# First layer's loop on Trainium2: K^T V over token tiles, with V taken inside or behind the loop, and gate logits per tile or per four tiles

## The chip, the core and the metric

The kernel runs on one core of one Trainium2 chip. The metric is device time in microseconds (us) of one execution, as the median of several runs. A core has five engines[...]: TensorE (PE in the profile, its weight loads PEld), VectorE (DVE), ScalarE (ACT), GpSimd (POOL) and SyncE (SP). They meet through semaphores. In this kernel SP issues nearly all DMA transfers. SBUF is the on-chip memory with 128 partitions, PSUM the accumulators that TensorE writes[...].

## The reference, cut to what matters

Two transformer layers over 2048 tokens of width 512, all in float32. The change lies in the first layer, in what is summed over all tokens before its main stage can start:

```python
xn = _layernorm(x)
k = heads(xn @ k_w.T + k_b);  v = heads(xn @ v_w.T + v_b)      # 16 heads of 32
kp = elu(k) + 1
kv = einsum('bhsd,bhse->bhde', kp, v)                          # sums over tokens
z  = einsum('bhsd,bhd->bhs', qp, kp.sum(axis=2))
attn = einsum('bhsd,bhde->bhse', qp, kv) / (z + EPS)
probas = sigmoid(x2 @ Wg.T)                                    # 16 experts, x2 = xn
_, idx = top_k(probas + biases, 8)
```

Linear attention needs one 32x32 matrix per head (kv) and the sum of kp. The mixture of experts needs, per token, the 8 highest of 16 gates. Only kv's diagonal blocks (a head with itself) are used, so the kernel computes a 128x128 block for four heads and multiplies it with a block-diagonal mask. Because v is linear in xn, the sum over tokens of kp^T v equals (sum of kp^T xn) V^T plus (sum of kp)^T v_b.

## The kernel before

Tokens are cut into NT = 16 tiles of P = 128; D = 512 is cut into NC = 4 chunks of 128; TB = 512 tokens make one of NTB = 4 blocks. Python code emits the instructions; a scheduler of the framework orders them per engine by its own estimates, and tile pools with a fixed number of buffers add the waits for a buffer's last reader. So the order on an engine is not exactly that of the source.

The first stage is the loop `for t in range(NT)` (L194 to L266). Per tile:

- VectorE takes layernorm statistics for four tiles ahead (`stats`, L72, L73, L76, L77) and writes xn (L224). GpSimd adds the output bias ob to x (L228), and SP stores that to DRAM as the residual.
- TensorE transposes xn in four pieces (tr, L100); ScalarE copies the result to xnT (L107).
- TensorE forms pk = xn K^T (L236): four matmuls of 512 columns. The profile counts eight, since each float32 matmul is issued twice here. VectorE adds the bias (kk, L238), takes min(kk, 0) (ke, L252), ScalarE takes the exponential (L253), VectorE forms elu + 1 (kk again, L254).
- TensorE forms pv in the same way (L241); VectorE adds its bias into vv (L244), which has a column of ones behind each group of 128, set by GpSimd (L243).
- TensorE forms pg (L257), gate logits with 16 columns, and adds kk^T vv to four PSUM accumulators kv of 128x129 (L259); the last column collects the sum of kp.
- `experts_of` turns the logits into a sigmoid and into each expert's rank among the 16: three short operations (L180, L181, L183) and five of 256 elements (L188 to L192) on VectorE.

Behind the loop VectorE masks kv into bd and the sums into bdz (L270 to L273). Then a new stage opens with other PSUM pools: query projections (pq, L305), a latent projection (pl, L329), the expert weights from the ranks (`expert_weights`), transposes of the weights (wp, L376), and `folded`, which multiplies bd with the output weights. A PSUM bank can be taken by the new stage when its old tile has been read.

[...]four banks for kv, two for tag "mm" (pk, pv), two for tag "tr" (tr, pg). Working SBUF tiles (xn, kk, ke and so on) have two buffers each, x has eight. SP's queue takes the loads in the order of the source: x of tile 0, k_wT, x of tile 1, kb, v_wT, vb, x of tile 2, WgT, rb, x of tile 3, ob, then x of tiles 4 to 7 and the weights of the later stages.

Of the kernel before, what the change touches and what calls it, by code (L numbers as in the profile page):

```python
# [19 lines left out]
P = 128  # L20
T = 2048
NT = T // P
# [16 lines left out]
def two_layer_kernel(ctx: ExitStack, tc: tile.TileContext, a: dict, out: bass.AP):  # L39
# [27 lines left out]
    def load(eng, dst, src):  # L67
        eng.dma_start(out=dst, in_=src)
# [34 lines left out]
    def vcopy(o, i):  # L103
        V.tensor_copy(o, i)
# [12 lines left out]
    with ExitStack() as l0:  # L117
# [15 lines left out]
        with ExitStack() as p1:  # L133
            w1 = p1.enter_context(tc.tile_pool(name="w1", bufs=1))
            wk1 = p1.enter_context(tc.tile_pool(name="wk1", bufs=2))
            ps_kv = p1.enter_context(tc.tile_pool(name="ps_kv", bufs=1, space=PSUM))
            ps1 = p1.enter_context(tc.tile_pool(name="ps1", bufs=2, space=PSUM))

            kc = "(c p) o -> p c o"
            x = {}  # L140

            def load_x(t):
                x[t] = wk1.tile([P, D], F32, tag="x", name=f"x_{t}", bufs=8)
                load(nc.sync, x[t], a["x"][t * P : (t + 1) * P, :])


            load_x(0)
            k_wT = weight("k_wT", [P, NC, D], a["k_wT"].rearrange(kc, p=P), w1)
            load_x(1)
            kb = weight("kb", [P, D], a["k_b"].partition_broadcast(P), w1)  # L150
            v_wT = weight("v_wT", [P, NC, D], a["v_wT"].rearrange(kc, p=P), w1)
            vb = weight("vb", [P, D], a["v_b"].partition_broadcast(P), w1)
            load_x(2)
            WgT = weight("WgT", [P, NC, E], a["WgT"].rearrange(kc, p=P))
            rb = weight("rb", [P, E], a["rbias"].partition_broadcast(P), w1)
            load_x(3)
            ob = weight("ob", [P, D], a["o_b"].partition_broadcast(P), w1)
            bmask = const([P, P], "bmask", w1)
            make_block_diagonal(nc, bmask, HD)
            tie = const([P, E, E], "tie", w1)  # L160
            G.memset(tie, 1.0)
            G.affine_select(
                out=tie, in_=tie, pattern=[[1, E], [-1, E]], compare_op=ALU.is_gt, fill=0.0,
                base=0, channel_multiplier=0,
            )
            mv = const([P, NT, 2], "mv", w1)
            rstd = const([P, NT], "rstd", w1)
            def stats(lo, hi):
                for t in range(lo, hi):
                    layernorm_stats(wk1, mv[:, t, :], x[t], f"st_{t}")  # L170
                rsqrt_into(rstd[:, lo:hi], mv[:, lo:hi, 1], eps5)

            stats(0, 1)
            stats(1, 4)

            def experts_of(t, pg):

                V.tensor_scalar_add(prob[:, t, :], pg, 1.0)  # L180
                V.reciprocal(prob[:, t, :], prob[:, t, :])  # L181
                sc = wk1.tile([P, E], F32, tag="sc", name=f"sc_{t}")
                V.tensor_tensor(sc, prob[:, t, :], rb, ALU.add)  # L183
                other = sc.unsqueeze(1).to_broadcast([P, E, E])
                own = sc.unsqueeze(2).to_broadcast([P, E, E])
                gt = wk1.tile([P, E, E], F32, tag="gt", name=f"gt_{t}")
                eq = wk1.tile([P, E, E], F32, tag="eq", name=f"eq_{t}")
                V.tensor_tensor(gt, other, own, ALU.is_gt)  # L188
                V.tensor_tensor(eq, other, own, ALU.is_equal)
                V.tensor_tensor(eq, eq, tie, ALU.mult)  # L190
                V.tensor_tensor(gt, gt, eq, ALU.add)
                V.tensor_reduce(rank[:, t, :], gt, AX.X, ALU.add)  # L192

            kv = [ps_kv.tile([P, P + 1], F32, tag=f"kv{g}", name=f"kv{g}") for g in range(NC)]  # L194
            for t in range(NT):
                tok = slice(t * P, (t + 1) * P)
                xt = xnT[t // 4][:, :, t % 4 * P : (t % 4 + 1) * P]
                if t % 4 == 0 and t + 4 < NT:
                    for u in range(t + 4, t + 8):
                        load_x(u)  # L200
                    stats(t + 4, t + 8)
                if t == 0:
                    q_b = weight("q_b", [P, NC], a["q_b"])

                    q_wT = weight("q_wT", [P, NC, D], a["q_wT"].rearrange(kc, p=P))
                    WdT = weight("WdT", [P, NC, LAT], a["WdT"].rearrange(kc, p=P))
                    sw1T = weight("sw1T", [P, NC, HID], a["sw1T"].rearrange(kc, p=P))
                    swgT = weight("swgT", [P, NC, HID], a["swgT"].rearrange(kc, p=P))
                    rw1T = weight("rw1T", [P, E, HID], a["rw1T"])
                    rwgT = weight("rwgT", [P, E, HID], a["rwgT"])  # L210
                    rw2T = weight(
                        "rw2T", [P, 2, E, LAT], a["rw2T"].rearrange("(b p) e l -> p b e l", p=P)
                    )
                    o_wT = weight("o_wT", [P, NC, D], a["o_wT"].rearrange(kc, p=P))
                    sw2T = weight("sw2T", [P, 2, D], a["sw2T"].rearrange(kc, p=P))
                    WuT = weight("WuT", [P, D], a["WuT"])
                    wr = weight("wr", [P, D], a["w_router"].partition_broadcast(P))
                    for j in range(2):
                        load(
                            nc.sync, w_qk[:, :, j * D : (j + 1) * D],  # L220
                            a["w_qkv"][:, j * D : (j + 1) * D].rearrange(kc, p=P),
                        )
                xn = wk1.tile([P, D], F32, tag="xn", name=f"xn_{t}")
                V.tensor_scalar(  # L224
                    xn, x[t], mv[:, t, 0:1], rstd[:, t : t + 1], ALU.subtract, ALU.mult
                )

                G.tensor_tensor(x[t], x[t], ob, ALU.add)  # L228
                load(nc.sync, res_d[tok, :], x[t])
                transpose4(  # L230
                    ps1, lambda c: xn[:, c * P : (c + 1) * P], xt, f"tr_{t}", scopy
                )

                pk = ps1.tile([P, D], F32, tag="mm", name=f"pk_{t}")
                for c in range(NC):
                    PE.matmul(pk, xt[:, c, :], k_wT[:, c, :], start=c == 0, stop=c == NC - 1)  # L236
                kk = wk1.tile([P, D], F32, tag="kk", name=f"kk_{t}")
                V.tensor_tensor(kk, pk, kb, ALU.add)  # L238
                pv = ps1.tile([P, D], F32, tag="mm", name=f"pv_{t}")
                for c in range(NC):  # L240
                    PE.matmul(pv, xt[:, c, :], v_wT[:, c, :], start=c == 0, stop=c == NC - 1)  # L241
                vv = wk1.tile([P, NC, P + 1], F32, tag="vv", name=f"vv_{t}")
                G.memset(vv[:, :, P : P + 1], 1.0)  # L243
                V.tensor_tensor(  # L244
                    vv[:, :, 0:P],
                    pv.rearrange("p (g e) -> p g e", g=NC),
                    vb.rearrange("p (g e) -> p g e", g=NC),
                    ALU.add,
                )

                ke = wk1.tile([P, D], F32, tag="ke", name=f"ke_{t}")
                V.tensor_scalar_min(ke, kk, 0.0)  # L252
                S.activation(ke, ke, AF.Exp)  # L253
                V.scalar_tensor_tensor(kk, kk, 0.0, ke, ALU.max, ALU.add)  # L254
                pg = ps1.tile([P, E], F32, tag="tr", name=f"pg_{t}")
                for c in range(NC):
                    PE.matmul(pg, xt[:, c, :], WgT[:, c, :], start=c == 0, stop=c == NC - 1)  # L257
                for g in range(NC):
                    PE.matmul(  # L259
                        kv[g], kk[:, g * P : (g + 1) * P], vv[:, g, :],  # L260
                        start=t == 0, stop=t == NT - 1,
                    )

                eg = wk1.tile([P, E], F32, tag="eg", name=f"eg_{t}")
                S.activation(eg, pg, AF.Exp, scale=-1.0)
                experts_of(t, eg)  # L266


            for g in range(NC):
                V.tensor_tensor(bd[:, g, :], kv[g][:, 0:P], bmask, ALU.mult)  # L270
                ks = wk1.tile([P, 1], F32, tag="ks", name=f"ks_{g}")
                vcopy(ks, kv[g][:, P : P + 1])
                V.tensor_scalar_mul(bdz[:, g, :], bmask, ks)  # L273

        with ExitStack() as p3:
# [1030 lines left out]
```

## Time and profile before

| what | value |
|---|---|
| median of 3 runs | 1873.57 us (1873.55 to 1880.08) |
| profiled execution, its own time | 1869.43 us |
| span in the profile | 1867.7 us |
| mean granted clock of TensorE | 0.97 |
| first loop, first transpose to last kv | 7.1 to 161.5 us |
| VectorE busy from 100 to 155 us | 37.7 of 55 us |
| ScalarE busy from 100 to 155 us | 8.3 of 55 us |
| GpSimd busy from 100 to 155 us | 5.3 of 55 us |
| first query projection of the next stage starts | 162.89 us |

The profile shows one execution. A timeline row gives start, length, engine, line of the kernel, operation, output and inputs, shapes and a count; in brackets stands how long the engine was idle before it and which engine's instruction released it. [...]start to start is what a group costs. The span begins with the first instruction and is somewhat shorter than the execution's time.

### The profile page before, as it was taken

The numbers are of one execution on the slowest core, as the hardware profiler recorded it, in microseconds if no ns is written. First come the engines' busy times: TensorE is split into PE (matmuls) and PEld (weight loads), VectorE is DVE, ScalarE is ACT, GpSimd is POOL, SyncE is SP. The second block draws the span as 40 slices with busy tenths as digits, with TensorE's granted clock in tenths as the row PEclk, the third lists the DMA queues.
The fourth block names the chain that finished last, engine by engine and source line by source line (L and its number), as shares of the span: only waits on it lengthen the run. The fifth ranks groups of instructions, "written<-read, shape, count | busy, mean of one in ns | idle before, by whom it ended". The sixth has DMA issues, their size and how long they took to land. (4 is left out here: it accounts for less than half of the span.)

```text
span 1867.7 us, 20604 instructions
## 1 busy us (share of the span) xinstructions
PE 1740.5 (93%) x8120; PEld 767.4 (41%) x8120; DVE 1008.1 (54%) x1445; ACT 573.7 (31%) x923; POOL 497.2 (27%) x372
## 2 busy tenths in 40 slices
PE   7999999999999999868988887999999999999999
PEld 4555444344444333323433333454565333333333
DVE  6775645436445343696666564575555455444344
ACT  3212334233233243111111111142100366446463
POOL 2110000100100110333344431331000467458583
PEclk9999999999999999989999897999999899999999
DMA  9301001210213130100001004311132300110100
GB/s 362 128 29 43 23 28 39 85 34 29 72 53 74 33 109 23 62 23 23 23 23 29 26 12 149 122 51 68 46 111 92 91 1 1 35 57 1 46 1 35
DMA packets 61810, 107.12 MB, mean 57 GB/s; under 512 B 12209, under 2 KB 13745, under 8 KB 61201
## 3 DMA queue, kind: packets, MB, share of 16 engines
q1 hardware_dynamic: 55280, 104.01, 16.7%
q0 software_dynamic: 1152, 1.21, 0.4%
q8 instruction: 63, 1.03, 0.2%
q10 hardware_dynamic: 5280, 0.59, 0.2%
q14 instruction: 35, 0.28, 0.0%
HBM read 84.14 MB, written 21.65 MB: 57 GB/s over the span
## 5 line engine op out<-in xcount | busy, mean ns | idle before, releaser
L527 DVE TENSOR_REDUCE mx<-pa 128x4 f32<-128x1536 f32 (+3 forms) x144 | 252.9, 1756 | 178.2 <-PE pa L523 83.8
L1210 POOL TENSOR_TENSOR acc<-acc,pt 128x1024 f32<-128x1024 f32 (+3 forms) x126 | 253.8, 2047 | 122.1 <-ACT pt L1137 75.8
L1137 ACT ACTIVATE pt<-ps 128x1024 f32<-128x1024 f32 (+3 forms) x208 | 182.2, 923 | 138.1 <-DVE ps L1128 86.4
L515 PE MATMUL pa<-kT,qT 32*128 32x384 f32 (+3 forms) x1152 | 158.0, 562 | 47.5 <-DVE mx L527 39.3
L1104 PE MATMUL ps<-qT,kT 32*128 32x512 f32 (+3 forms) x1152 | 162.0, 535 | 8.6 <-ACT pt L1137 8.1
L93 POOL TENSOR_TENSOR xr<-xr,xn 128x512 f32<-128x512 f32 x16 | 27.0, 1697 | 493.6 <-DVE xn L87 493.6
L424 PE MATMUL acc<-h,rw2T 128*128 128x512 f32 x256 | 135.3, 616 | 14.9 <-DVE h L290 14.3
L288 ACT ACTIVATE r_e<-eg 128x512 f32<-128x512 f32 x128 | 75.8, 594 | 222.4 <-PE eg L419 202.4
L782 PE MATMUL p<-w_qk,xnt 128*128 128x512 f32 x256 | 129.7, 631 | 8.3 <-ACT xnt L107 8.3
L290 DVE TENSOR_TENSOR h<-ea,r_e 128x512 f32<-128x512 f32 x128 | 87.0, 686 | 87.2 <-ACT r_e L289 59.9
L421 PE MATMUL ea<-xw,rw1T 128*128 128x512 f32 x256 | 130.7, 592 | 0.0
L419 PE MATMUL eg<-xl,rwgT 128*128 128x512 f32 x256 | 130.7, 592 | 0.0
L1128 DVE TENSOR_TENSOR ps<-ps,maskT 128x256 f32<-128x256 f32 (+1 forms) x144 | 68.3, 514 | 100.3 <-PE ps L1111 97.2
L1104 PEld LDWEIGHTS ps<-qT,kT 32*128 32x128 f32 x1152 | 62.2, 186 | 116.5 <-issue 55.4
L515 PEld LDWEIGHTS pa<-kT,qT 32*128 32x128 f32 x1152 | 52.0, 191 | 138.3 <-DVE mx L527 88.0
L1177 PE MATMUL av<-pt,v 128*32 128x512 f32 (+3 forms) x1024 | 102.3, 485 | 0.2
L415 DVE TENSOR_TENSOR xw<-xw,xl 128x512 f32<-128x512 f32 x64 | 43.9, 685 | 94.9 <-DMA xw<-w_d 94.9
L1219 DVE RECIPROCAL sm<-sm 128x128 f32<-128x128 f32 x64 | 61.8, 965 | 57.4 <-PE sm L1191 56.0
L424 PEld LDWEIGHTS acc<-h,rw2T 128*128 128x128 f32 x256 | 43.4, 188 | 95.5 <-DVE h L290 79.4
L289 ACT ACTIVATE r_e<-r_e 128x512 f32<-128x512 f32 x128 | 80.2, 629 | 6.4 <-issue 1.9
L650 POOL TENSOR_TENSOR t<-qk,cosg 128x1024 f32<-128x1024 f32 x15 | 35.3, 2354 | 161.7 <-DVE qk L645 145.5
L421 PEld LDWEIGHTS ea<-xw,rw1T 128*128 128x128 f32 x256 | 48.6, 190 | 61.2 <-issue 60.8
(278 smaller groups left out, 2542.2 us busy)
## 6 DMA issues: line engine op xcount, KB each, us to landing
xw<-w_d SPq DMA_DIRECT2D x64, 256.0 KB, 3.2
x<-in_x SPq DMA_DIRECT2D x16, 256.0 KB, 4.3
res_d<-x SPq DMA_DIRECT2D x16, 256.0 KB, 2.3
xr<-res_d SPq DMA_DIRECT2D x16, 256.0 KB, 4.8
xn_d<-xn SPq DMA_DIRECT2D x16, 256.0 KB, 2.4
res_d<-xr SPq DMA_DIRECT2D x16, 256.0 KB, 2.0
xnq<-xn_d SPq DMA_DIRECT2D x16, 256.0 KB, 2.9
v_d<-vt SPq DMA_DIRECT2D x16, 256.0 KB, 2.9
```

Source lines behind the costliest of these rows:

```text
L289: S.activation(r, r, AF.Square)
L290: V.tensor_tensor(dst, pa, r, ALU.mult)
L419: PE.matmul(pg, rwgT[:, e, hb], xl, start=True, stop=True)
L421: PE.matmul(pa, rw1T[:, e, hb], xw, start=True, stop=True)
L424: PE.matmul(acc, rw2T[:, j, e, :], h, start=e == 0 and j == 0, stop=e == E - 1 and j == 1,)
L515: PE.matmul(pS[:, h, : w * P], qT[r, g, i * P : (i + 1) * P], kT[r, g, ks], start=True, stop=not (edge or last),)
L527: V.tensor_reduce(mx[:, g, :, c], pS[:, :, : w * P], AX.X, ALU.max)
L782: PE.matmul(pj, xnt[:, c, :], w, start=c == 0, stop=c == NC - 1)
L1104: PE.matmul(pS[h // 2][:, h % 2, t0 * P - q0 : (t1 + 1) * P - q0], kT[r, g, kb * P : (kb + 1) * P], qT[r, g, t0 * P : (t1 + 1) * P], start ...
L1137: S.activation(pT[:, :, :n], pS[hp][:, :, :n], AF.Exp)
L1177: PE.matmul(self.av[h * HD : (h + 1) * HD, t0 * P - o : (t1 + 1) * P - o], vs[kb // 4][:, kb % 4, hs], got[h // 2][:, h % 2, t0 * P - q0 : ...
L1210: eng.tensor_tensor(part, part, got[hp][:, :, : q1 - q0], ALU.add)
```

## The change

Four things change.

1. The loop no longer forms v. It accumulates gx = kk^T xn, four PSUM tiles of 128x512, over all tiles (`gathered`). A tile's gx is emitted one tile later, behind the next tile's pk. The sum of kp is kept by GpSimd (ksum, one add per tile). xn gets three buffers instead of two.
2. Behind the loop, gx is copied out (gs), transposed (trg, gT) and multiplied with the V weights, only in the 128 columns that a group of four heads needs. ksum's column sum comes from a matmul with a column of ones. The V bias enters as vb times that sum, then the mask.
3. Gate logits come per block of four tiles (`gates`): each of the four chunks of xnT goes through its own group of 32 columns of the array with weights padded from 16 to 32 columns, the four partial sums land on four groups of partitions of one PSUM tile, ScalarE copies them out, and matmuls with a 0/1 matrix `fold` add them up and turn them to tokens on partitions. Sigmoid and bias are then done for four tiles at once, the ranking per tile as before. The gates of the last block are emitted behind the loop.
4. The loads of v_wT and vb move behind x of tile 3; WgT is zeroed by GpSimd first.

```diff
@@ -148,12 +148,15 @@
             k_wT = weight("k_wT", [P, NC, D], a["k_wT"].rearrange(kc, p=P), w1)
             load_x(1)
             kb = weight("kb", [P, D], a["k_b"].partition_broadcast(P), w1)
+            load_x(2)
+
+            WgT = const([P, NC, HD], "WgT", w1)
+            G.memset(WgT, 0.0)
+            load(nc.sync, WgT[:, :, 0:E], a["WgT"].rearrange(kc, p=P))
+            rb = weight("rb", [P, E], a["rbias"].partition_broadcast(P), w1)
+            load_x(3)
             v_wT = weight("v_wT", [P, NC, D], a["v_wT"].rearrange(kc, p=P), w1)
             vb = weight("vb", [P, D], a["v_b"].partition_broadcast(P), w1)
-            load_x(2)
-            WgT = weight("WgT", [P, NC, E], a["WgT"].rearrange(kc, p=P))
-            rb = weight("rb", [P, E], a["rbias"].partition_broadcast(P), w1)
-            load_x(3)
             ob = weight("ob", [P, D], a["o_b"].partition_broadcast(P), w1)
             bmask = const([P, P], "bmask", w1)
             make_block_diagonal(nc, bmask, HD)
@@ -163,6 +166,15 @@
                 out=tie, in_=tie, pattern=[[1, E], [-1, E]], compare_op=ALU.is_gt, fill=0.0,
                 base=0, channel_multiplier=0,
             )
+            ones = const([P, 1], "ones", w1)
+            G.memset(ones, 1.0)
+            ksum = const([P, D], "ksum", w1)
+            G.memset(ksum, 0.0)
+
+            fold = const([P, E], "fold", w1)
+            V.tensor_reduce(
+                fold, ident.rearrange("p (c e) -> p e c", c=4)[:, 0:E, :], AX.X, ALU.add
+            )
             mv = const([P, NT, 2], "mv", w1)
             rstd = const([P, NT], "rstd", w1)
             def stats(lo, hi):
@@ -173,25 +185,53 @@
             stats(0, 1)
             stats(1, 4)
 
-            def experts_of(t, pg):
-
-
-
-                V.tensor_scalar_add(prob[:, t, :], pg, 1.0)
-                V.reciprocal(prob[:, t, :], prob[:, t, :])
-                sc = wk1.tile([P, E], F32, tag="sc", name=f"sc_{t}")
-                V.tensor_tensor(sc, prob[:, t, :], rb, ALU.add)
-                other = sc.unsqueeze(1).to_broadcast([P, E, E])
-                own = sc.unsqueeze(2).to_broadcast([P, E, E])
-                gt = wk1.tile([P, E, E], F32, tag="gt", name=f"gt_{t}")
-                eq = wk1.tile([P, E, E], F32, tag="eq", name=f"eq_{t}")
-                V.tensor_tensor(gt, other, own, ALU.is_gt)
-                V.tensor_tensor(eq, other, own, ALU.is_equal)
-                V.tensor_tensor(eq, eq, tie, ALU.mult)
-                V.tensor_tensor(gt, gt, eq, ALU.add)
-                V.tensor_reduce(rank[:, t, :], gt, AX.X, ALU.add)
-
-            kv = [ps_kv.tile([P, P + 1], F32, tag=f"kv{g}", name=f"kv{g}") for g in range(NC)]
+            def gates(b):
+
+
+
+
+                parts = ps1.tile([P, TB], F32, tag="mm", name=f"pgp_{b}")
+                for c in range(NC):
+                    PE.matmul(
+                        parts[c * HD : (c + 1) * HD, :], WgT[:, c, :], xnT[b][:, c, :],
+                        start=True, stop=True, skip_group_check=True,
+                    )
+                gp = wk1.tile([P, TB], F32, tag="gp", name=f"gp_{b}", bufs=1)
+                scopy(gp, parts)
+                pg = ps1.tile([P, 4, E], F32, tag="tr", name=f"pg_{b}")
+                for i in range(4):
+                    PE.matmul(
+                        pg[:, i, :], gp[:, i * P : (i + 1) * P], fold, start=True, stop=True
+                    )
+
+                four = slice(4 * b, 4 * b + 4)
+                pr = prob[:, four, :]
+                S.activation(pr, pg, AF.Exp, scale=-1.0)
+                V.tensor_scalar_add(pr, pr, 1.0)
+                V.reciprocal(pr, pr)
+                sc = wk1.tile([P, 4, E], F32, tag="sc", name=f"sc_{b}", bufs=1)
+                V.tensor_tensor(sc, pr, rb.unsqueeze(1).to_broadcast([P, 4, E]), ALU.add)
+                for i in range(4):
+                    other = sc[:, i, :].unsqueeze(1).to_broadcast([P, E, E])
+                    own = sc[:, i, :].unsqueeze(2).to_broadcast([P, E, E])
+                    gt = wk1.tile([P, E, E], F32, tag="gt", name=f"gt_{b}_{i}")
+                    eq = wk1.tile([P, E, E], F32, tag="eq", name=f"eq_{b}_{i}")
+                    V.tensor_tensor(gt, other, own, ALU.is_gt)
+                    V.tensor_tensor(eq, other, own, ALU.is_equal)
+                    V.tensor_tensor(eq, eq, tie, ALU.mult)
+                    V.tensor_tensor(gt, gt, eq, ALU.add)
+                    V.tensor_reduce(rank[:, 4 * b + i, :], gt, AX.X, ALU.add)
+
+
+            gx = [ps_kv.tile([P, D], F32, tag=f"gx{g}", name=f"gx{g}") for g in range(NC)]
+
+            def gathered(t, kk, xn):
+                for g in range(NC):
+                    PE.matmul(
+                        gx[g], kk[:, g * P : (g + 1) * P], xn, start=t == 0, stop=t == NT - 1
+                    )
+
+            before = None
             for t in range(NT):
                 tok = slice(t * P, (t + 1) * P)
                 xt = xnT[t // 4][:, :, t % 4 * P : (t % 4 + 1) * P]
@@ -220,7 +260,7 @@
                             nc.sync, w_qk[:, :, j * D : (j + 1) * D],
                             a["w_qkv"][:, j * D : (j + 1) * D].rearrange(kc, p=P),
                         )
-                xn = wk1.tile([P, D], F32, tag="xn", name=f"xn_{t}")
+                xn = wk1.tile([P, D], F32, tag="xn", name=f"xn_{t}", bufs=3)
                 V.tensor_scalar(
                     xn, x[t], mv[:, t, 0:1], rstd[:, t : t + 1], ALU.subtract, ALU.mult
                 )
@@ -236,40 +276,48 @@
                     PE.matmul(pk, xt[:, c, :], k_wT[:, c, :], start=c == 0, stop=c == NC - 1)
                 kk = wk1.tile([P, D], F32, tag="kk", name=f"kk_{t}")
                 V.tensor_tensor(kk, pk, kb, ALU.add)
-                pv = ps1.tile([P, D], F32, tag="mm", name=f"pv_{t}")
-                for c in range(NC):
-                    PE.matmul(pv, xt[:, c, :], v_wT[:, c, :], start=c == 0, stop=c == NC - 1)
-                vv = wk1.tile([P, NC, P + 1], F32, tag="vv", name=f"vv_{t}")
-                G.memset(vv[:, :, P : P + 1], 1.0)
-                V.tensor_tensor(
-                    vv[:, :, 0:P],
-                    pv.rearrange("p (g e) -> p g e", g=NC),
-                    vb.rearrange("p (g e) -> p g e", g=NC),
-                    ALU.add,
-                )
 
                 ke = wk1.tile([P, D], F32, tag="ke", name=f"ke_{t}")
                 V.tensor_scalar_min(ke, kk, 0.0)
                 S.activation(ke, ke, AF.Exp)
                 V.scalar_tensor_tensor(kk, kk, 0.0, ke, ALU.max, ALU.add)
-                pg = ps1.tile([P, E], F32, tag="tr", name=f"pg_{t}")
+                G.tensor_tensor(ksum, ksum, kk, ALU.add)
+                if before is not None:
+                    gathered(*before)
+                before = t, kk, xn
+                if t % 4 == 3 and t < NT - 1:
+                    gates(t // 4)
+            gathered(*before)
+            gs = []
+            for g in range(NC):
+                gs.append(wk1.tile([P, D], F32, tag="gs", name=f"gs_{g}", bufs=4))
+                (vcopy if g % 2 else scopy)(gs[g], gx[g])
+            gates(NTB - 1)
+
+
+
+            def turned_g(g):
+                gT = wk1.tile([P, NC, P], F32, tag="ke", name=f"gT_{g}")
+                transpose4(
+                    ps1, lambda c: gs[g][:, c * P : (c + 1) * P], gT, f"trg_{g}",
+                    scopy if g % 2 else vcopy,
+                )
+                return gT
+
+            gT = turned_g(0)
+            for g in range(NC):
+                cols = slice(g * P, (g + 1) * P)
+                this, gT = gT, turned_g(g + 1) if g < NC - 1 else None
+                kv = ps1.tile([P, P + 1], F32, tag="mm", name=f"kv_{g}")
                 for c in range(NC):
-                    PE.matmul(pg, xt[:, c, :], WgT[:, c, :], start=c == 0, stop=c == NC - 1)
-                for g in range(NC):
                     PE.matmul(
-                        kv[g], kk[:, g * P : (g + 1) * P], vv[:, g, :],
-                        start=t == 0, stop=t == NT - 1,
-                    )
-
-                eg = wk1.tile([P, E], F32, tag="eg", name=f"eg_{t}")
-                S.activation(eg, pg, AF.Exp, scale=-1.0)
-                experts_of(t, eg)
-
-
-            for g in range(NC):
-                V.tensor_tensor(bd[:, g, :], kv[g][:, 0:P], bmask, ALU.mult)
+                        kv[:, 0:P], this[:, c, :], v_wT[:, c, cols], start=c == 0, stop=c == NC - 1
+                    )
+                PE.matmul(kv[:, P : P + 1], ksum[:, cols], ones, start=True, stop=True)
                 ks = wk1.tile([P, 1], F32, tag="ks", name=f"ks_{g}")
-                vcopy(ks, kv[g][:, P : P + 1])
+                vcopy(ks, kv[:, P : P + 1])
+                V.scalar_tensor_tensor(bd[:, g, :], vb[:, cols], ks, kv[:, 0:P], ALU.mult, ALU.add)
+                V.tensor_tensor(bd[:, g, :], bd[:, g, :], bmask, ALU.mult)
                 V.tensor_scalar_mul(bdz[:, g, :], bmask, ks)
 
         with ExitStack() as p3:
```

Around the transposes, the copies and pk nothing changes, nor in any later stage.

## The prediction

> **What bounds the kernel now.** I read the page's busy table first, then TensorE's timeline over the first layer's loop, then VectorE's and GpSimd's, then the hand-over to the next stage.
>
> ```profile
> PE 1740.5 (93%) x8120; PEld 767.4 (41%) x8120; DVE 1008.1 (54%) x1445; ACT 573.7 (31%) x923; POOL 497.2 (27%) x372
> ```
>
> TensorE is busy 93% of the span. One loop tile in its timeline (start, length, engine, line, operation):
>
> ```profile
> 115.10 1.06 PE L259 MATMUL kv<-vv,kk 128*128 128x129 f32 x8
> 116.00 3.64 PE L236 MATMUL pk<-k_wT,xnT 128*128 128x512 f32 x8
> 119.48 3.60 PE L241 MATMUL pv<-v_wT,xnT 128*128 128x512 f32 x8
> 122.91 0.96 PE L257 MATMUL pg<-WgT,xnT 128*128 128x16 f32 x8
> 123.72 0.64 PE L100 MATMUL tr<-ident,xn 128*128 128x128 f32 x4
> 124.19 1.06 PE L259 MATMUL kv<-vv,kk 128*128 128x129 f32 x8
> ```
>
> No row has an idle time in brackets: this loop is bound by TensorE. From start to start: kv 0.90, pk 3.48, pv 3.43, pg 0.81, tr 0.47, together 9.09 us a tile. The loop ends here:
>
> ```profile
> 160.38 1.13 PE L259 MATMUL kv<-vv,kk 128*128 128x129 f32 x8
> 162.89 5.37 PE L305 MATMUL pq<-xnT,q_wT 128*128 128x512 f32 x8 [1.38 <-issue]
> 168.09 3.60 PE L329 MATMUL pl<-xnT,WdT 128*128 128x512 f32 x8
> ```
>
> The next stage starts at 162.89, 1.4 us behind the last kv. Its first group takes 5.2 us instead of 3.43, at a granted clock of 0.68. In a row by windows (busy time of TensorE, its weight loads, VectorE, ScalarE and GpSimd, then clock, DMA share and GB/s):
>
> ```profile
> 163.00:168.30 5.30, 5.30 (x9) 2.27 (x10) 2.90 (x12) 0.00 (x0) 0.00 (x0) 0.68 0.44 134
> ```
>
> On VectorE and GpSimd I read the chain from pk to a finished kk, the gates, and what a GpSimd operation does to them:
>
> ```profile
> 97.87 1.18 DVE L183 TENSOR_TENSOR sc<-prob,rb 128x16 f32<-128x16 f32 x1
> ...
> 137.86 0.69 DVE L238 TENSOR_TENSOR kk<-pk,kb 128x512 f32<-128x512 f32 x1 [0.28 <-PE pk L236]
> 138.59 0.43 DVE L252 TENSOR_SCALAR ke<-kk 128x512 f32<-128x512 f32 x1
> 139.77 0.69 DVE L254 SCALAR_TENSOR_TENSOR kk<-kk,ke 128x512 f32<-128x512 f32 x1 [0.76 <-ACT ke L253]
> ...
> 161.44 0.41 DVE L188 TENSOR_TENSOR gt<-sc 128x256 f32<-128x256 f32 x1
> 161.77 0.42 DVE L189 TENSOR_TENSOR eq<-sc 128x256 f32<-128x256 f32 x1
> ```
>
> ```profile
> 97.75 1.27 POOL L228 TENSOR_TENSOR x<-x,ob 128x512 f32<-128x512 f32 x1 [7.78 <-DVE xn L224]
> ```
>
> From pk's end (137.66) to kk's second write (140.46) is 2.8 us, 2.87 with the signal to TensorE. Independent gate operations follow every 0.33 to 0.34 us, dependent ones every 0.46. The tiny sc took 1.18 us because GpSimd was adding ob; elsewhere (142.87) it takes 0.17.
>
> [...]eight 128x512 instructions of 32 columns, in four groups, follow the eight before them after 0.88 us, where eight full-width ones take 3.43.
>
> ```profile
> 1507.79 1.07 PE L1177 MATMUL av<-acc,v 128*32 128x512 f32 x8
> 1508.67 1.04 PE L1191 MATMUL sm<-acc,ones_f 128*32 128x512 f32 x8
> ```
>
> [...]Here 1.4 us of idle between short matmuls already led to 0.68.
>
> **The loop.** Per tile pv (3.43), kv (0.90) and pg (0.81) go. gx comes: four matmuls kk x xn of 512 columns, priced as pv, 3.43. Per four tiles come four column-group matmuls (0.88, from av) and four fold matmuls (0.81, as pg). So four tiles cost 4 x (0.47 + 3.48 + 3.43) + 0.88 + 0.81 = 31.2 us instead of 36.4: 5.2 a block, 20.6 in four blocks, if TensorE never waits.
>
> Waits, from the built order of instructions, walked with the durations above:
> - The copy of xnT takes 0.7 us from tr's end. Before, kv stood between; now gx's first matmul (0.86) usually does. It doesn't before tiles 5, 9 and 13 (behind a gates block) nor 10: 4 x about 0.8 lost; and pk of tile 1 waits 0.3.
> - The first gx of a tile stands behind three gx and a tr of the next round: 2.57 + 0.47 = 3.04 us, against 2.87 for kk. It just fits; behind it queue pk and everything later.
> - The fold waits for a ScalarE copy (0.7). After blocks 0 and 2 a gx covers it, after block 1 nothing: 0.8.
> - VectorE now gets the gates of four tiles in one piece: add, reciprocal and sc 0.6, then 20 interleaved operations x 0.34 = 6.8. The next tile's kk, ke and the xn two tiles on queue behind. In block 0 gates start near 40.1 and kk of tile 4 near 47.2, while TensorE has gx, tr and pk until 50.5. Then the add of ob (1.27) locks out kk's last operation: ready about 51.1, 0.7 late. The same in block 2. In block 1 four layernorm statistics join, yet xn of tile 10 (about 83.2) still meets its tr (83.9).
> - ksum, 16 new GpSimd adds of 1.27, lies beside other work[...].
>
> New waits sum to 3.2 + 0.3 + 0.8 + 1.4 = 5.7. Old ones were alike: from the end of the first pk (14.47) to the last kv (161.4) are 146.9 us, of which 15 x 9.09 + 5.1 = 141.5 are work, so 5.4 idle, 2.1 of it for the statistics of tiles 1 to 3. Those come earlier now: v_wT and vb (1.25 MB) move behind x of tiles 2 and 3 in SP's queue, so xn of tile 1 is ready near 13, before the first pk ends. x of tiles 4 to 7 has the same transfers ahead as before. The 64 KB of WgT's wider tile is only memory.
>
> After: 15 x (0.47 + 3.48) + 16 x 3.43 + 4 x 0.88 + 0.9 (the last group-matmuls are split around gx) + 3 x 0.81 = 121.0, plus 5.7 = 126.7: the loop ends near 141.2 by this sum, 140.6 in the walk, which charges pk 3.43 to 3.48. I take 140.6: 20.8 us earlier than 161.4.
>
> **The tail takes most of it back.** At 140.6: ScalarE copy and fold to 142.3, Exp to 142.6, add and reciprocal to 143.1, VectorE's copy of the first transposed gx to 143.7. TensorE transposes and does the first two kv by about 146.5. The third kv needs the third transposed copy, and its PSUM buffer back from the first bd. Both stand on VectorE behind 19 gate operations of tiles 12 to 15: 143.9 + 6.5 = 150.4, ks and copy to 151.1, last reduction and bd to 151.7. TensorE is idle about 5 us there, so I charge half clock: kv 3 and 4 take 1.9 us each instead of 1.1 (eight of 0.11 and two for ks), to 155.7. pq starts at once: its bank was a gx bank, long read. I give pq 4.4, between 3.43 (warm by then) and 5.2 (still cold): end 160.1, before 168.1. The expert weights' order behind pq is unchanged, and rank is ready by 154, ahead of its transposes.
>
> Sum: 20.8 - (15.1 - 1.5) + 0.8 = 8.0 us gained (the tail is 15.1 now, 1.5 before; pq is 0.8 shorter). From pq on the order of every engine is the same: the rest only moves. Profiled execution: 1869.43 -> 1861.4, span 1867.7 -> 1859.7. The median of the runs, 1873.57, stands 4.1 higher; I take the same 8.0 off: **1865.6**. A comparison of this kernel can't tell less than about 0.5% (9.4 us) from no change; the forecast lies just inside that.
>
> **Unknown costs.** gx: kk as stationary operand, between pv's 3.43 and 3.48 as pk (0 to 0.8 in sum). Group matmuls: 0.88 to 3.43 if they don't overlap. Tail: half clock costs 0 to 3.4 in all (kv and pq), and the gate step may be 0.46 (+2.3). Lock: [...]some 4 us more if it catches an operation of each block's chain twice.
>
> **Rivals.**
> - Faster: waits behind gates hide, the lock costs nothing, the clock stays up: 8.0 + 1.4 + 1.6 + 1.0 = 12, time 1861.6. For it: the old tail shows only 1.4 us from kv to pq. Against: the order puts the gates ahead of the copy. 0.36 for anything beyond 9.4.
> - Column groups run one after another: 4 x 2.55 = 10.2 lost, time 1875.8. Against it: the av rows, same type and shape. 0.05.
> - Small gain: gates step 0.46 and locks add up: 8.0 - 2.3 - 4 = 1.7, time 1872. 0.12.
> - Slower, one mechanism: kk is late in each tile. Its cover is 0.17 us (3.04 against 2.87). If ksum's and ob's adds, both on GpSimd behind kk and xn, hold ke and kk's last operation in every tile, each lateness counts about 12 times: at 0.84 us the gain is gone, at 1.6 it is slower by 0.5%; both adds in the chain (2.5) give 1893.6. Against: by the walk these adds end before the next pk does. 0.07.
> - The forecast, a gain of 5 to 9.4: 0.40.
>
> Faster 0.36, same 0.57 (forecast, small gain, serial groups), slower 0.07. The range from 1859.5 to 1874 leaves out slower, serial groups and the end of faster. The forecast's own range is 1864 to 1869.
>
> **What would show it.** A tile period near 7.4 between gates, no idle before gx above 0.2 us outside them; the four group matmuls within 1 us; TensorE idle some 5 us before the third kv, released by VectorE's copy of gT; pq starting near 155. Wrong if gx waits for kk in most tiles, or if the next stage starts before 151 or after 160.

## The result

| | before | after |
|---|---|---|
| median of the runs made together | 1873.55 us (1868.85 to 1880.08) | 1863.01 us (1855.82 to 1869.61) |
| profiled execution, its own time | 1869.43 us | 1855.82 us |
| span in the profile | 1867.7 us | 1854.1 us |
| first query projection starts | 162.89 us | 158.56 us |
| latent projection starts | 168.09 us | 162.72 us |
| fold of the output weights (pw) starts | 177.3 us | 172.0 us |

The ratio after to before is 0.994, with a 95% interval from 0.9925 to 0.9955: a gain of 10.5 us, between 8.4 and 14. The forecast was 1865.6 us, a gain of 8.0.

Below, "the fold" as a place in time is the start of pw, the fold of the output weights; the fold inside the loop's gates is the multiplication with the 0/1 matrix. "Half clock" is a stretch in which the profile's record of the granted TensorE clock shows 0.5.

The busy table of the page, after:

```profile
PE 1728.6 (93%) x7984; PEld 749.5 (40%) x7984; DVE 984.0 (53%) x1402; ACT 576.1 (31%) x919; POOL 519.1 (28%) x375
```

TensorE has 136 instructions and 11.9 us of busy time less, VectorE 24.1 us less, GpSimd 21.9 us more (ksum). TensorE's timeline of the changed first stage (start, length, engine, line, operation, and in brackets the idle time before it with its releaser):

```profile
20.65 3.70 PE L230 MATMUL gx<-xn,kk 128*128 128x512 f32 x8 [0.34 <-DVE kk L283]
...
37.68 1.06 PE L195 MATMUL pgp<-xnT,WgT 128*32 128x512 f32 x8
38.68 1.12 PE L230 MATMUL gx<-xn,kk 128*128 128x512 f32 x2
...
56.90 3.68 PE L276 MATMUL pk<-k_wT,xnT 128*128 128x512 f32 x8
60.41 2.74 PE L230 MATMUL gx<-xn,kk 128*128 128x512 f32 x6
62.99 0.60 PE L100 MATMUL tr<-ident,xn 128*128 128x128 f32 x4
63.43 1.04 PE L230 MATMUL gx<-xn,kk 128*128 128x512 f32 x2
64.30 3.66 PE L276 MATMUL pk<-k_wT,xnT 128*128 128x512 f32 x8
...
138.31 3.70 PE L230 MATMUL gx<-xn,kk 128*128 128x512 f32 x8
141.94 1.06 PE L195 MATMUL pgp<-xnT,WgT 128*32 128x512 f32 x6
143.69 1.07 PE L203 MATMUL pg<-fold,gp 128*128 128x16 f32 x8 [0.69 <-ACT gp L107]
...
154.27 2.07 PE L313 MATMUL kv<-v_wT,gT 128*128 128x128 f32 x8 [3.12 <-DVE bd L319]
...
158.56 4.33 PE L353 MATMUL pq<-xnT,q_wT 128*128 128x512 f32 x8
162.72 3.60 PE L377 MATMUL pl<-xnT,WdT 128*128 128x512 f32 x8
```

A TensorE row overlaps the next by some 0.17 us (56.90 + 3.68 against 60.41). A tile now takes 7.40 us from pk to pk (64.30 - 56.90), where it took 9.09. The eight group instructions take 1.00 us (37.68 to 38.68). The loop's last group matmul ends at 143.0; before, its last kv ended at 161.5. Then the tail takes most of it back: the third kv stands still for 3.12 us and runs at half clock (the granted clock is 0.50 from 153.1 to 159.8 us), and the next stage begins only 4.3 us, its second group 5.4 us earlier than before.

What the third kv waits for is seen on VectorE, behind the ranks of the last four tiles (rows from 146.54 on, one every 0.33 us, not shown):

```profile
50.41 1.60 DVE L283 SCALAR_TENSOR_TENSOR kk<-kk,ke 128x512 f32<-128x512 f32 x1 [0.30 <-ACT ke L282]
...
152.95 0.68 DVE L104 COPY gT<-trg 128x512 f32<-128x512 f32 x1
153.55 0.41 DVE L223 TENSOR_REDUCE rank<-gt 128x16 f32<-128x256 f32 x1
153.88 0.34 DVE L319 SCALAR_TENSOR_TENSOR bd<-vb,ks,kv 128x128 f32<-128x128 f32 x1
```

The copy gT and the first bd, which frees the PSUM buffer that the third kv takes, both come behind the ranks; the profile names bd (154.22) as what released it. The first row of the view belongs to the loop: it is the long kk at the end of block 0's gates, 1.60 us in place of 0.69. GpSimd was adding ob just then:

```profile
50.20 1.27 POOL L268 TENSOR_TENSOR x<-x,ob 128x512 f32<-128x512 f32 x1 [9.50 <-DVE xn L264]
```

This is what the prediction calls the lock: an operation of VectorE that took longer beside GpSimd's add of ob. The pair comes once more in block 2 (kk 1.60 us at 117.28, the add 1.27 us at 117.06). What couples the two wasn't shown.

Two questions are left by this pair of traces. The spans differ by 13.6 us, the medians by 10.5, the entries of the next stage by 5.4 only, and from there on every engine has the same instructions in the same order. Where do the rest come from? And which part of the change earns what?

### The profile page after: what moved, and what is told of

Read it like the earlier page. It is cut to its first block, busy times and chain, and to the rows that moved or that the text cites. A ratio compares the mean times of both kernels' runs of the same rounds, so it can differ in the third digit from the quotient of the medians.

```text
span 1854.1 us, 20264 instructions
## 1 busy us (share of the span) xinstructions
PE 1728.6 (93%) x7984; PEld 749.5 (40%) x7984; DVE 984.0 (53%) x1402; ACT 576.1 (31%) x919; POOL 519.1 (28%) x375
## 5 line engine op out<-in xcount | busy, mean ns | idle before, releaser
L698 POOL TENSOR_TENSOR t<-qk,cosg 128x1024 f32<-128x1024 f32 x15 | 35.3, 2353 | 158.2 <-DVE qk L693 141.9
L467 PEld LDWEIGHTS eg<-xl,rwgT 128*128 128x128 f32 x256 | 48.6, 190 | 61.2 <-issue 60.0
```

The lines of the kernel that those rows point to most:

```text
L467: PE.matmul(pg, rwgT[:, e, hb], xl, start=True, stop=True)
```

## The experiments

All kernels were timed in rounds together with the kernel before. Milestones are from each kernel's own trace.

### Halves of the change

**gx alone.** The loop gathers gx and takes the V weights behind it; the gates stay tile by tile.

```diff
-                if t % 4 == 3 and t < NT - 1:
-                    gates(t // 4)
+                pg = ps1.tile([P, E], F32, tag="tr", name=f"pg_{t}")
+                for c in range(NC):
+                    PE.matmul(pg, xt[:, c, :], WgT[:, c, :], start=c == 0, stop=c == NC - 1)
...
+                experts_of(t, eg)
...
-            gates(NTB - 1)
```

> Only gx: v leaves the loop as in the change, gates stay per token tile as before. Theory A (the walk of instructions: the loop's gain is the removed kv and pv minus gx, and the four-tile gates give back in the tail what they save): a tile costs 0.47 + 3.48 + 0.81 + 3.43 = 8.2 us, kk has 3.85 us of cover, the tail has no gates in it and takes some 8 us; the next stage's first matmul starts near 151 to 153 us (before 162.9, the change 158.6), and the run is 10 to 14 us faster than before, so at least as fast as the whole change. Theory B (both parts give a share and gates in four column groups are needed for it): the first matmul starts later than 158.6, and the run lies between before and the change.

**Gates alone.** Four tiles' gates at once, pv, vv and kv in the loop as before.

```diff
-                for c in range(NC):
-                    PE.matmul(pg, xt[:, c, :], WgT[:, c, :], start=c == 0, stop=c == NC - 1)
...
-                experts_of(t, eg)
+                if t % 4 == 3:
+                    gates(t // 4)
```

> Only the gates: four tiles at once in column groups, V inside the loop as before. Theory A: the loop saves 4 x (3.24 - 1.7) = 6.2 us of TensorE, but VectorE's gates of four tiles come in one piece ahead of the next kk and vv, and TensorE waits for them; the next stage starts 1 to 5 us earlier than before, and the run is between 5 us faster and 3 us slower. Theory B: the run is 5 us faster or more.

Measured: gx alone 1860.59 us, ratio 0.9941 (0.9917 to 0.9966); gates alone 1881.38 us, ratio 1.0047 (1.0024 to 1.0069). The tail of gx alone, on TensorE:

```profile
152.74 3.68 PE L329 MATMUL pq<-xnT,q_wT 128*128 128x512 f32 x8
```

Its loop is longer than the change's (8.28 us a tile), yet the next stage starts at 152.7, 5.8 us before the change's: no block of ranks stands in VectorE's queue, no kv waits but the first (1.32 us for VectorE's copy of gT), and the granted clock is 1.00 from 36 to 150 us. Gates alone show what a block of gates does where kk feeds the same tile's kv:

```profile
144.38 4.54 PE L262 MATMUL pk<-k_wT,xnT 128*128 128x512 f32 x6 [1.97 <-DVE kk L264]
```

The 20 rank operations hold kk until 143.65, 5.6 us behind its pk, and TensorE runs out of work. The first expectation was met in full; the second was wrong for both theories, the loss (7.5 us against the shared 1873.87) being larger than either allowed. In the whole change, where kk feeds a gx one tile later, the same block of gates costs a gx 0.24 us (a pk of 3.78 us in place of 3.54, at 48.28 and 115.15): beside the one-tile delay the four-tile gates are bearable, without it they weren't.

The moved loads and xn's third buffer were in every kernel with gx, and in none without; what they are worth alone wasn't measured.

### Where the last block's gates stand

**Behind the V part**, and **ahead of tile 15's pk**:

```diff
-            gates(NTB - 1)
...
                 V.tensor_scalar_mul(bdz[:, g, :], bmask, ks)
+            gates(NTB - 1)
```

and, in the same way,

```diff
+                if t == NT - 1:
+                    gates(NTB - 1)
                 pk = ps1.tile([P, D], F32, tag="mm", name=f"pk_{t}")
...
-            gates(NTB - 1)
```

> The change with the last block's gates emitted behind the V part, so that VectorE does the copies and bd first. Theory A: TensorE's idle time before the third kv (3.1 us) and the waits for the gate copies (1.4 us) go, the kv matmuls run at the full clock, the next stage starts near 151 us instead of 158.6; the ranks come later and hold back the transposes of the expert weights by about 2 us. 4 to 7 us faster than the change. Rival (the tail is set by other waits, the transposes and copies of gx): within 2 us of the change.

> The change with the last block's gates emitted ahead of the last tile's pk. Theory A: VectorE's gates then stand ahead of the last kk, the last gx starts some 5 us late (near 144 us), and the tail behind it runs without gates: the next stage starts near 155 us, 3 to 4 us faster than the change. Rival (gates in the tail are hidden anyway): within 1 us of the change or slower by the late gx.

Measured: behind 1859.76 us, ratio 0.9928 (0.9901 to 0.9956); ahead 1863.24 us, ratio 0.9943 (0.9919 to 0.9966). TensorE with the gates behind:

```profile
151.01 3.68 PE L353 MATMUL pq<-xnT,q_wT 128*128 128x512 f32 x8
...
161.67 3.39 PE L424 MATMUL wp<-ident,rank 128*16 128x128 f32 x16 [3.54 <-DVE rank L418]
```

The tail is gone: pq at 151.0 as expected, no kv but the first waits (0.51 us), and the four take 0.89 to 1.00 us to the next row, where the change's third and fourth take 1.87 and 1.84. The 7.6 us come back in part as a wait of 3.54 us of the rank transposes, and in the transposes themselves (3.2 us to the next row, 1.7 in the change); the fold starts at 169.0, 3.0 before the change's, and the median is 3.3 below the change's, which was taken in another round: between the two theories, and not clear of noise, since the intervals of the two ratios overlap. With the gates ahead, the wait moved to the last gx:

```profile
144.78 6.73 PE L230 MATMUL gx<-xn,kk 128*128 128x512 f32 x8 [5.32 <-DVE kk L285]
```

kk of tile 15 queues on VectorE behind the ranks until 141.94, and behind the idle of 5.32 us this gx takes 6.6 us to the next row instead of 3.5. pq starts at 158.2: no gain, where 3 to 4 us were expected; the rival of that expectation held.

**Ranks later**: the edit is made in the kernel with the gates behind; the second query projection comes ahead of the transposed ranks.

```diff
             next(steps)
             next(steps)
-            expert_weights()
             next(steps)
+            expert_weights()
             folded()
```

> The change with the last block's gates behind the V part, and the transposed ranks behind the second query projection in place of ahead of it. Theory A: the first query projection at 151 us as with the gates behind alone, TensorE's wait of 3.5 us for the ranks gone (the second projection covers it), the fold of the output weights at about 165.5 us in place of 169.0, and a median about 3 us below that of the gates-behind version (1859.8), so about 1856.5. Rival B: the transposes wait as long as before for the ranks, since VectorE takes the second projection's result first: no gain, within 1 us of 1859.8.

Measured: 1854.43 us, ratio 0.9907 (0.9882 to 0.9932). The repeat, on one chip with the change and gx alone:

> The best version once more, on the same chip as the whole change: gates of the last block behind the V part and the transposed ranks behind the second query projection. Theory A (the time follows the start of the fold of the output weights, 164.3 against 172.0 in the change): 6 to 9 us faster than the change and within 2 us of the gx-only half. Rival B (its median of 1854.4 came with a higher mean clock of its six runs, 0.972): 2 us or less faster than the change.

Measured: 1855.81 us, ratio 0.9904 (0.9881 to 0.9927). TensorE in the repeat:

```profile
157.57 3.60 PE L353 MATMUL pq<-xnT,q_wT 128*128 128x512 f32 x8
161.37 1.91 PE L424 MATMUL wp<-ident,rank 128*16 128x128 f32 x16 [0.20 <-DVE rank L418]
```

The projection covers the ranks: 0.20 us of wait in place of 3.54, though the fold then waits 1.16 us for ScalarE's copy of bd. This is the fastest version: 7.0 us below the change measured beside it (1862.85), as theory A said, and 4.8 below gx alone, which it had put within 2.

### GpSimd's sum of kp

```diff
-                G.tensor_tensor(ksum, ksum, kk, ALU.add)
```

> Leaves out the sum of the kernel features over the tiles (GpSimd's addition into ksum), so the divisors of the attention and the bias term of its matrix are not computed rightly; all else is as in the change. Theory A[...]: the maximum-and-add on VectorE at 50 and 117 us falls from 1.60 to about 0.69 us, the waits of 0.2 to 0.3 us before gx there go, the first query projection starts 0.5 to 1.5 us earlier than the change's 158.6, and the median is 0 to 2 us below the change's. Rival B (the addition slows VectorE in every tile): tile period well below 7.39, entry more than 5 us earlier.

Measured: 1864.3 us, ratio 0.9958 (0.9943 to 0.9972), no better than the change; pq starts at 158.6 as in the change. VectorE at the same place:

```profile
50.41 1.59 DVE L283 SCALAR_TENSOR_TENSOR kk<-kk,ke 128x512 f32<-128x512 f32 x1 [0.30 <-ACT ke L282]
```

The long kk is still there without ksum's add: it goes with the add of ob (1.26 us from 50.19 on), as the prediction had it, not with ksum, as the expectation put it. Sixteen GpSimd adds cost nothing that can be seen.

### Does the rest only move?

Six matmuls of 128x512 ahead of the first query projection, in the change and in the kernel before:

```diff
                     pq = mm(f"pq_{b}_{g}")
+                    for _ in range(6 if (b, g) == (0, 0) else 0):
+                        PE.matmul(
+                            pq, q_wT[:, 0, 0:P], xnT[b][:, 0, :], start=True, stop=True
+                        )
```

> The change with six more 128x512 matmuls into the first query projection's tile ahead of it (overwritten, so nothing else differs): TensorE gets 5.2 us more to do just where the next stage begins (0.87 us each at full clock). Theory A (the rest of the kernel only moves, whatever its entry time): the latent projection starts 4.3 to 5.2 us later than the change's 162.7, and the median of the runs is 4 to 6 us above the change's. Rival B (the entry moves work that waits for VectorE, ScalarE or DMAs there and is absorbed): median within 2 us of the change's. Rival C[...]: median off by more than 3 us from theory A's, to either side.

> The kernel before with the same six matmuls ahead of the first query projection. Theory A: the median is 4 to 6 us above the kernel before's, the same step as with the changed kernel. Rival B: within 2 us. Rival C: off by more than 3 us from theory A[...].

Measured: the change so delayed 1867.2 us, ratio 0.9976 (0.9961 to 0.999), its fold at 177.0 (5.0 later than without); the kernel before so delayed 1877.12 us, ratio 1.0023 (1.0011 to 1.0034), its fold at 180.6 (3.3 later: here the six matmuls take 5.2 us and the first projection 3.4, while before's first projection takes 5.2, at a granted clock of 0.51 from 163.2 to 166.6 us). The median of before rose by 5.4 us over 1871.75, measured beside it. The change wasn't in this round: its median rises by 4.2 over 1863.01 from another round, by about 6.7 if the ratios 0.994 and 0.9976 are compared. So a delay at this place goes through to the end about one to one in both kernels, and a gain should too. It isn't exact for single executions: gates alone has its fold 15.7 us later than before (193.0), and its profiled execution is 11.4 us longer. The lasting difference beyond 5.4 us isn't explained by the later stages merely moving.

### What else the kernel before loses

**Placement**: the kernel before, with WgT in the pool of the first layer, as the change has it.

```diff
-            WgT = weight("WgT", [P, NC, E], a["WgT"].rearrange(kc, p=P))
+            WgT = weight("WgT", [P, NC, E], a["WgT"].rearrange(kc, p=P), w1)
```

> The kernel before with the gate weights allocated in the pool that is freed after the first layer (as the changed kernel has them), nothing else. Theory A (the placement is worth nothing): within 1.5 us of the kernel before. Rival B (about 4 us of the changed kernel's gain, those which its trace up to the latent projection does not show, come from the place of its buffers): 3 to 5 us faster than before.

**The change and gx alone once more**, unaltered, on the same chip:

> The changed kernel once more, beside the same runs of the kernel before as the three others. Theory A (its gain is what it gains up to the fold of the output weights, 5.4 us, and the rest of the 10.5 us was the scatter of the clock between runs): 5 to 8 us faster than before, the mean granted clock of its runs within 0.001 of that of before. Rival B (a lasting difference in the rest of the kernel): 9 to 12 us faster again.

> The half of the change that gathers kk times the normalized tile, with the gates left tile by tile as in the kernel before, once more, now on the same chip as the whole change. Theory A (the gates half costs more in the tail than it saves in the loop): 3 to 6 us faster than the whole change, by its fold of the output weights at 165.5 against 172.0. Rival B (the two are alike): within 2 us of it.

Measured: placement 1873.07 us, ratio 1.0 (0.998 to 1.002), so nothing that shows (the interval is 3.7 us to either side). The change again 1862.85 us, ratio 0.9943 (0.992 to 0.9967), against 1873.54 for before: 10.7 us, so rival B of its expectation holds and the 10.5 us weren't chance. The mean granted clock of its runs was 0.9693, that of before 0.9659. Over the runs of all kernels 0.001 of mean clock goes with 1.6 us, so this difference is worth about 5 us (an estimate from these runs): about half of the gain goes with less time at half clock. gx alone again 1860.63 us, ratio 0.9929 (0.9905 to 0.9953): 2.2 us below the change, between its two theories, with intervals that overlap.

The placement kernel's trace shows one way in which the old loop can lose more. It has the loop of the kernel before, but its first query projection starts at 167.65 and its fold at 181.9, 4.8 and 4.6 us later than in the trace of before. The difference arises at the first kv. TensorE's timeline of the kernel before, and of the placement kernel:

```profile
21.01 1.13 PE L259 MATMUL kv<-vv,kk 128*128 128x129 f32 x8 [2.14 <-DVE mv L73]
```

```profile
21.74 2.06 PE L259 MATMUL kv<-vv,kk 128*128 128x129 f32 x8 [2.63 <-DVE mv L73]
```

The view by windows of 20 to 31 us (busy time of TensorE, its weight loads, VectorE, ScalarE, GpSimd, then clock, DMA share, GB/s), again before and then placement:

```profile
20.00:31.00 11.00, 9.32 (x36) 5.29 (x37) 10.12 (x20) 4.59 (x7) 4.15 (x4) 1.00 1.07 412
```

```profile
20.00:31.00 11.00, 8.58 (x19) 4.95 (x20) 8.82 (x18) 4.70 (x6) 4.25 (x4) 0.53 1.05 405
```

In the placement kernel the granted clock is 0.53 over these 11 us, about 10 us at half clock, half of which is lost: the kv group takes 2.06 us instead of 1.13, and the next pk 6.36 instead of 3.70. The four traces with the old loop order: behind an idle of 1.74 (before, delayed) and 2.14 (before) the kv group takes 0.97 and 0.96 us to the next row, behind 2.47 (gates alone) and 2.63 (placement) 1.67 and 1.86. Four traces give no threshold, and what sets off the half clock wasn't shown.

With gx the first tile's gather stands behind the next tile's transpose and pk, and x of tiles 2 and 3 is loaded earlier. In that stretch TensorE waits at most 0.34 us in the change and 1.1 us in gx alone, and the granted clock is 1.00 from 10 to 36 us in four traces of kernels with gx (both of the change, the first of gx alone, the repeat with the ranks later). Which of the two does it, the order or the loads, wasn't taken apart.

Taking the placement kernel's trace as another execution of the old loop, and the change's second one (1864.41 us, fold at 171.1, near its median), the folds lie 10.8 us apart, about what the medians differ by. Taking the trace of before, they lie 6.2 apart. But in the old loop delayed the first kv takes 0.97 us to the next row, and that execution (1877.11 us) lies on its kernel's median (1877.12): it loses the time further on, with a mean granted clock of 0.966 over its span of 1875.3 us, about 128 us at half clock. So the half clock at 20 us can be a part of the lasting 5 us, and not all of it in each execution; how often it comes wasn't counted, and the cause of the 5 us stays open. The kernel before with the statistics of tiles 1 to 3 behind the first kk would test it, and wasn't measured.

## Why the prediction was right, and by how much

**The order of work and the waits: right.** The period of 7.4 us, pk waiting 0.67 to 0.68 for the copy of xnT at 48.28, 81.85, 86.66 and 115.15 (tiles 5, 9, 10 and 13), the fold waiting 0.70 in block 1, the long kk beside the add of ob in blocks 0 and 2 (1.60 us at 50.41 and 117.28), the four groups within 1 us and kv 3 released by VectorE: each came where the walk had put it. Outside these, gx waits only at its first matmul. The long kk cost a gx 0.24 us each time instead of 0.7. The slower rival (kk late in each tile) and the serial column groups are out.

**The loop's sum: 2.4 us too small.** From the end of the first pk to the end of the last group matmul (14.47 to 143.0) it took 128.5 us, TensorE busy for 124.4, where 121.0 of work and 5.7 of waits were priced. The idle was 1.6 less, the work 3.4 more; the other 0.6 is that 140.6, from the walk, was taken in place of the sum's 141.2. On average gx measured 3.51 a tile instead of the 3.43 taken from pv, and pk 3.55 instead of 3.48. A cut by transposes costs nothing more (six and two gx take 2.58 + 0.86 = 3.44, from 60.41 on). What costs more is a run beside group matmuls (3.63 from 138.31 to 141.94; two gx 0.96 at 38.68) and a run after a wait (3.54 from 52.06), and pk takes 3.50 to 3.51 in a tile without gates; its average also holds the two waits of 0.24 for the long kk. The group matmuls took 1.0 instead of 0.88. Small errors of price, many times over.

**The tail: right to 0.5 us.** 143.0 to 158.56 is 15.6 us, forecast 15.1. The gate operations follow every 0.33 us, kv 3 waits 3.1 us instead of about 5, released by bd, the last link of the chain that the prediction gave for it. The clock was half already at the first kv (0.50 from 146.2 to 149.6 us, after 0.69 and 0.68 us of idle among short matmuls), so the first kvs took longer (1.71 and 1.04 us to the next row) and the wait shrank; kv 3 and 4 ran at half clock (0.50 from 153.1 to 159.8 us) as charged, an estimate from the 0.68 that before shows behind 1.4 us of idle. In the second trace of the change, where the first kvs take 0.91 and 0.89 us, the wait is 4.62 us and pq starts at 158.4: the chain on VectorE sets the end, not TensorE. pq itself took 4.16 instead of 4.4.

Together: 2.4 + 0.5 - 0.2, about 2.6 late at the latent projection, 162.7 for 160.1, and a gain of 5.4 where 8.0 were summed.

**"From pq on the order of every engine is the same: the rest only moves": the step that failed for the profiled pair.** The order is the same, and a delay put there does move the end by about as much. But executions differ in the rest. In the clock's record of the traces, the time at half clock from the fold to the last matmul is 109.2 us in before and 99.0 in the change's first trace; over the profiled executions of all kernels the mean granted clock lies between 0.963 and 0.973. The stretch itself (1685.9 and 1677.6 in the first pair) less half of that is 1631 and 1628 us. So half clock accounts for about 5.1 of the 8.3 us between the rests of the first pair; of the remaining 3, about 1 may be one longer operation in a later layernorm, if it lies on the chain that ends last, which wasn't shown: the same VectorE product (L90, near 350 us) took 1.76 us in before and 0.69 in the change's first trace (GpSimd was working on xr beside it in both, from 353.45 and 347.77 on), 1.77 in its second. The change's first trace was a lucky one: its time of 1855.82 is 7.2 below the median.

**The median was right in part by luck.** The prediction took 8.0 off the median as it did off the profiled execution. By its terms the change earns 5.4 there. The measured 10.5 needs about 5 more, for which the prediction has no term; by the runs' mean clocks it goes with less time at half clock. The trace of before, 4.1 under its median, doesn't show what the old loop loses in other executions. So the 2.6 us by which the sum was too large were more than made up by a gain that wasn't forecast. At 1863.0 the result lies inside the range, 1 us outside the likeliest case's own range, and in the first rival's gain (over 9.4 us), but not by that rival's mechanism: the waits didn't hide, and the tail did run at half clock.

Open is also why gx alone, whose fold starts 5.6 to 6.5 us before the change's, is only 2.2 to 2.4 us faster, and not clear of noise. The mean granted clock of its two profiled executions is 0.968 and 0.968, that of the change's 0.970 and 0.969; four traces are too few to call this a cause.

## What to carry to other kernels

Work that doesn't feed the critical chain (here four tiles' ranks) should be emitted behind the chain's operations on the same engine and behind enough other TensorE work: moving the last gates and the ranks' transposes turned a 0.6% gain into 0.95%. One profile can be spared what others lose: with the same loop, a TensorE wait of 2.14 us went without half clock in one trace, and one of 2.63 went with about 10 us of it in another. When a loop is re-cut, price its groups by rows with the same neighbours: eight gx cost from 3.43 to 3.63 us by what stood around them, and such differences come once a tile.

## What the runs showed of the hardware that was not expected

- Within one kernel, executions differ by up to 19 us (1865.77 to 1884.68 in the placement kernel), and the time follows the mean granted clock: 1.6 us for each 0.001 over the runs of all kernels, close to the 1.9 that 0.001 of 1870 us is.
- In the clock records of before and of the change's first trace, half clock comes in 16 stretches each, of 3.4 to 27.3 us in steps of 3.41 (the last is cut off by the end), and their starts lie whole multiples of 3.41 us apart. In the change's tail one began at 146.2 us, 0.5 us into an idle of 0.68 among short matmuls.
- Four-column-group matmuls of 128x512 take 1.00 us for eight instructions, where 0.88 was taken from a later stage and eight of full width take 3.43.
